# Linear attention's product with Wo in sixteen 32x32 tiles of the array, and two steps of the gated attention moved later

## The chip, the cores and the metric

The kernel runs on one core of a Trainium2 chip. The metric is the device time in microseconds of one execution; for the kernel before it is the median of three runs. Engines are named as the profile names them: PE is TensorE's matmul, PEld its weight load, DVE is VectorE, ACT is ScalarE, POOL is GpSimd, SP is SyncE. Times such as "at 93.2" are microseconds from the start of the profiled span.

## The reference, cut to what matters

Two layers on x of 2 x 1024 rows and 512 columns, all fp32: linear attention, a gated feed-forward with 4-bit weights, gated (chunked) linear attention, a feed-forward on the top half of the rows; a layer norm of the residual sum after each. The change touches the first and the third.

```python
# layer 0, linear attention: 16 heads of 32 columns
q = feature_map(proj(Wq))          # elu + 1, (b, h, t, d)
k = feature_map(proj(Wk))
v = proj(Wv)
kv = einsum('bhtd,bhte->bhde', k, v)
z = 1.0 / (einsum('bhtd,bhd->bht', q, k.sum(axis=2)) + 1e-06)
out = einsum('bhtd,bhde,bht->bhte', q, kv, z)
return out.reshape(b, t, c) @ Wo.T
...
# layer 1, gated attention: o comes from the chunked recurrence
go = o @ Wog.T + x @ Wig.T
on = o * rsqrt(mean(o * o) + EPS) * g_norm_w
return (on * silu(go)) @ Wo.T
```

## The kernel before, in words

Rows are worked in four blocks of 512 (two per batch), columns in four chunks of 128 (KC = 4). The kernel writes out the order of its matmuls by hand: generators are stepped by `run`, each step yields one or two products, and the lists given to `run` say what goes between them; `behind()` and `tc.issue_after` pin TensorE's order. On the other engines the compiler's scheduler orders the instructions, and each engine then runs its queue strictly in that order: an instruction that waits holds up all behind it.

**Linear attention** (first 230 us). `by_seven` (L304) makes a 512x512x512 projection with seven block products of 256 in place of eight (Strassen's scheme in Winograd's form): L315 is its matmul; the sums of blocks that it needs are `sums_of_weights` (L301) and VectorE operations at L322 to L324 and L339. One PSUM bank, `grow`, is added to by several products, so each reader of it has to be done before the next product may add. `elu1` (L270 to L272) is the feature map: two ScalarE passes and one on VectorE.

Per batch b, the kernel does not form v. It sums x^T k over the rows (`add_xk`, L366), a 512x512 array copied into G, and then:

- `values` (L417): Wv times G, only the four 128x128 blocks on the diagonal (four heads each), into the bank `vk`. VectorE multiplies it by a 0/1 mask, so that of each block only the four 32x32 squares of the heads remain (`vkm`, L420).
- `G_rows` (L430): for each chunk c one product of 128x128 by 128x512, `vkm[:, c]` with `Wo[:, c]`, into a bank `gp`; copies into G, two on VectorE and two on ScalarE (L431). G is now the weight that takes q to the output. Then VectorE makes the four block sums of G for the seven-product scheme (`sums_of_weights`, L301 again; tile names wdn, TG and T).
- `weigh` (L399 to L405): q is divided per row and head by q times the sum of k; six VectorE operations per 128 rows. The sum of k over the rows is spread over the partitions by a product with ones, and copied (`spread_ksum`, L391).
- `turned` (L446): q is transposed on TensorE in 128-column pieces (`qTp`, four transposes per 128 rows) and copied to `qT` by ScalarE.
- `o_products` (L461): qT times G by seven products, each added to the residual x by VectorE (L467). The sums S1, qS and A21 at L469 to L471 and A12 at L478 feed it.

Banks come from two rings of four or fewer: `mm` (projections) and `acc` (xk, qTp, gp, output products). Between these steps lies the unpacking of the 4-bit weights, one `job` at a time: a load on SyncE's queue, two VectorE operations (L236, L237; tile pk) and one ScalarE conversion (L240, tile wgu). For batch 1 the split of the next layer's input into two parts (`split_some`; x1Tp, x1Th by ScalarE, x1Tl by VectorE L211) lies there too. Wq arrives by DMA in the tile that the products read. `wdn` is the tile of the later feed-forward's down weights; its free chunks serve as room before it is filled.

**Gated attention** (545 to 745 us). Per block `scores`, `attend` and `gate` run. `gate` (L1180) makes go by seven products; L1215 and L1216 are two VectorE additions that empty its banks, L1224 another, `end` (L1194, L1197) applies silu and the norm weight. `finish_by_seven` (L1264, read by L1272) makes the product with the layer's own Wo (tile W1o) for the block before; the weight sums come from `sums_of_W1o` (four VectorE operations, L1241), the input sums from `sums_of_u` (L1249 to L1251). `gates.decayed` makes the decay factor of the second batch's keys: a product `ep` (L699) that needs ScalarE's logarithm l (L685), then exp (L702) and a VectorE product (L704); the next `scores` needs it for the states (`up`, L1112: one 128x32 by 128x512 product for each tile of rows, the results in four different strips of 32 partitions of one bank). The layer norm of a block takes row statistics on VectorE (L187, L188), a power on GpSimd (rs, L180) and the scaling on VectorE (L182). `x_sum` (L993) is a sum of the next block's input.

Of the kernel before, what the change touches and what calls it, by code (L numbers as in the profile page):

```python
# [21 lines left out]
P = 128  # L22
# [16 lines left out]
def _constants():  # L39
    t = np.arange(P)  # L40
    tt, ii = t[:, None], t[None, :]
    same = (tt // CH) == (ii // CH)
    mid = (ii // CH) * CH + CH // 2 - 1

    e1 = np.where(same & (tt > mid) & (tt <= ii), 1.0, 0.0)
    e1 -= np.where(same & (tt > ii) & (tt <= mid), 1.0, 0.0)
    e2 = np.where(ii < CH, (tt > ii) & (tt < CH), (tt >= CH) & (tt <= ii)) * 1.0
    e3 = (tt <= ii) * 1.0
    parts = {
        "ident": np.eye(P),  # L50
        "cm": -np.concatenate([e1, e2, e3], axis=1),
        "suf": -1.0 * (tt > ii),
        "caus": same & (tt <= ii),
        "tril": ii < tt,
        "heads": np.concatenate([(tt // 32) == (ii // 32), (tt // 32) == np.arange(4)[None, :]], axis=1),
        "one": np.ones((P, 1)),
        "place": tt + P * np.arange(4 * NB)[None, :],
        "mhalf": np.full((P, 4), -0.5),
    }
    at, n = {}, 0  # L60
    for name, a in parts.items():
        at[name] = (n, a.shape[1])
        n += a.shape[1]
    table = np.concatenate([np.asarray(a, np.float32) for a in parts.values()], axis=1)
    shift = (28 - 4 * (t % 8)).astype(np.int32)[:, None]
    return table, at, shift
# [6 lines left out]
def body(ctx: ExitStack, tc: tile.TileContext, a: dict, out: bass.AP):  # L73
# [13 lines left out]
    def bank(ring, name):  # L87
        i = rings[ring][turn_of[ring] % len(rings[ring])]
        turn_of[ring] += 1
        return psum.tile([P, 512], F32, tag=f"bank{i}", name=name)  # L90
# [3 lines left out]

    def acc_bank(name):
        return bank("acc", name)


    table = cpool.tile([P, _TABLE.shape[1]], F32, name="table")

    def const(name):
        at, n = _AT[name]
        return table[:, at : at + n]
# [11 lines left out]
    def load_w(dst, name):  # L115
        nc.sync.dma_start(out=dst, in_=a[name].rearrange("(k p) o -> p k o", p=P))
# [29 lines left out]
    nc.sync.dma_start(out=shift, in_=a["shift"])  # L146
    nc.sync.dma_start(out=table, in_=a["table"])
    load_x(1)
    load_w(Wq, "WqT")
    load_w(Wv, "WvT")  # L150
    load_w(Wo, "WoT")
    for blk in range(NB):
# [63 lines left out]
            nc.tensor.matmul(ps, lhs[:, k], w[:, k], start=start and k == 0, stop=stop and k == KC - 1)  # L216


    fp4 = ctx.enter_context(ExitStack())
    wfp4 = fp4.enter_context(tc.tile_pool(name="wfp4", bufs=1))  # L220
    wgu = wpool.tile([P, KC, 2 * I_FF], F32R, tag="big", name="wgu")
    wdn = wfp4.tile([P, NI, C], F32, name="wdn")
    gus = wfp4.tile([KC * FG, P], F16, name="gus")
    scale = wfp4.tile([P, KC * FG], F32, name="scale")
    s1 = ctx.enter_context(ExitStack())
    wk = s1.enter_context(tc.tile_pool(name="s1", bufs=2))
    dq = s1.enter_context(tc.tile_pool(name="dq", bufs=2))
# [25 lines left out]
            yield wdn[:, g], a["dn"][16 * g : 16 * (g + 1), :], a["dns"][g : g + 1, :], C  # L253

    to_unpack = unpacking()
    anchor = [None]

    def unpack_some(n):
# [6 lines left out]
    def elu1(dst, ps):  # L265

        e = wk.tile([P, C], F32, tag="e", name="e")
        if len(ps.shape) == 3:
            e = e.rearrange("p (r c) -> p r c", r=2)
        nc.scalar.activation(e, ps, AF.Relu, scale=-1.0)  # L270
        nc.scalar.activation(e, e, AF.Exp, scale=-1.0)
        anchor[0] = nc.vector.scalar_tensor_tensor(dst, ps, 0.0, e, ALU.max, ALU.add).ins  # L272


# [112 lines left out]
    def spread_ksum(b):  # L387

        sp_ = mm_bank("ksumb")
        with behind():  # L390
            last_pe[0] = nc.tensor.matmul(sp_, ones, ksum_of[b], start=True, stop=True).ins  # L391
        nc.scalar.copy(ksum_of[b], sp_)

    def weigh(blk, t):

# [14 lines left out]
    def values(b):  # L410

        vk = mm_bank("vk")
        with behind():
            for c in range(KC):
                cut = slice(c * P, (c + 1) * P)
                for k in range(KC):
                    ins = nc.tensor.matmul(vk[:, cut], Wv[:, k, cut], G_of[b][:, k, cut], start=k == 0, stop=k == KC - 1).ins  # L417
        last_pe[0] = ins
        vkm_of[b] = wk.tile([P, KC, P], F32, tag="vkm", name="vkm", bufs=1)
        nc.vector.tensor_mul(  # L420
            vkm_of[b],
            vk.rearrange("p (c d) -> p c d", c=KC),
            const("heads")[:, :P].unsqueeze(1).to_broadcast([P, KC, P]),
        )

    def G_rows(b):
        for c in range(KC):
            gp = acc_bank("gp")
            with behind():
                last_pe[0] = nc.tensor.matmul(gp, vkm_of[b][:, c], Wo[:, c], start=True, stop=True).ins  # L430
            (nc.scalar.copy if c % 2 else nc.vector.tensor_copy)(G_of[b][:, c], gp)  # L431

        room = wdn[:, 7:11] if b == 0 else place_w(3, "TG")
        rooms = slices(room, 0, 3)
        if b:

            rooms.append(pieces_of(wk.tile([P, 512], F32, tag="qT3", name="T3", bufs=1)))
        TG[b] = sums_of_weights(G_of[b], rooms), pieces_of(room[:, 3])
# [113 lines left out]
    def some_xk(blk, *part):  # L552
        return [lambda i=i: add_xk(blk, i) for i in part]
# [29 lines left out]
    for b in range(B):  # L583
        i, j = 2 * b, 2 * b + 1
        if b:
            run(
                k_products(i),
                turns(1, 0, 1) + job(1), job(1),
                turns(1, 2, 3) + some_o(1, 1) + job(1), some_o(1, 2) + job(1), some_o(1, 5) + job(1),
            )  # L590
        run(k_products(j), [], some_xk(i, 0, 1) + job(2), some_xk(i, 2) + job(1), some_xk(i, 3) + job(1), job(1 + b))
        if b == 0:
            Ts["q"] = sums_of_weights(Wq, slices(wdn, 0, 3))
        else:

            Tq = place_w(1, "Tq")
            for n in range(3):
                nc.scalar.copy(Tq[:, n], wdn[:, n])
            Ts["q"] = (*slices(Tq, 0, 2), Ts["q"][2], *slices(Tq, 2, 3))
            S_rooms[0] = pieces_of(Tq[:, 3])  # L600
        run(
            q_products(i, lambda t: weigh(i, t)), [],
            some_xk(j, 0, 1) + job(1 + b), some_xk(j, 2) + step(spread_ksum, b) + job(1), some_xk(j, 3) + job(1 + b),
        )
        if b == 0:
            xT[2] = load_xT(2)
        split = [step(split_some, n) if b else [] for n in range(4)]
        rings["free"] = (rings["sum"][(turn_of["sum"] + 1) % 2],)
        run(
            q_products(j, lambda t: None),  # L610
            step(values, b),
            turns(i, 0, 1) + split[0] + job(1 - b),
            step(G_rows, b) + split[1] + turns(i, 2, 3) + job(1 - b),
            some_o(i, 2) + split[2] + some_o(i, 1) + job(1 - b),
            step(all_free) + some_o(i, 1) + step(weigh, j, 0) + split[3] + some_o(i, 3) + step(weigh, j, 1) + some_o(i, 1),
        )
        if b == 0:
            xT[3] = load_xT(3)
# [447 lines left out]
    def scores(blk, gates, beside=None):  # L1066
# [7 lines left out]
        nc.tensor.transpose(tp[:, :P], of_tiles(gates.q, blk), ident)  # L1074
        nc.tensor.transpose(tp[:, P : 2 * P], of_tiles(gates.k, blk), ident)
        qp, kp = tp[:, :P], tp[:, P : 2 * P]
        own = const("heads")[:, P:]

        def over(x, n=P):
            return x.unsqueeze(1).to_broadcast([P, 4, n])  # L1080
# [163 lines left out]
    def sums_of_u():  # L1244

        A = uT[0].rearrange("p (m e) (s t) -> p m e s t", e=2, s=2)
        A11, A12, A21, A22 = (A[:, :, e, s] for s in range(2) for e in range(2))
        S1, S2 = (wk.tile([P, 512], F32, tag="sil", name=f"uS{i}", bufs=2).rearrange("p (m t) -> p m t", m=2) for i in range(2))
        nc.vector.tensor_add(S1, A21, A22)  # L1249
        nc.vector.tensor_sub(S2, S1, A11)  # L1250
        nc.vector.tensor_sub(A21, A11, A21)  # L1251
        return (A11, A12, A21, A22), (S1, S2)

    def finish_by_seven(blk, u, w):

# [398 lines left out]
        next(ending)  # L1654
    for blk in range(NB):
        if blk == 1 or blk == 2:
            sums = sums_of_u()
        if blk == 2:
            front(3, gates)
        if blk == 1:  # L1660
# [9 lines left out]
        if blk:  # L1670
            o_sum(blk)
            gating = gate(blk)
            if blk < 3:
                finishing = finish_by_seven(blk - 1, sums, W1o_sums)
                for n in range(2):
                    next(finishing)
                    next(gating)
                    if blk == 1 and n == 0:
                        with tc.issue_after(last_3[0]):
                            last_3[0] = gates.decayed(kd_room, jk.tile([P, 8, 32], F32, tag="junk", name="e3"))  # L1680
                next(finishing)
                scored = scored_rows(blk - 1)
            else:
                scored = finish(blk - 1)
                for _ in range(2):
                    next(gating)
# [6 lines left out]
            scores(blk + 1, gates)  # L1693
        if blk == 0:
            o_sum(0)
            with tc.issue_after(scored):
                W1o_sums = sums_of_W1o()
            nc.sync.dma_start(out=rw, in_=a["rw"].to_broadcast([P, C]))
            nc.sync.dma_start(out=b2, in_=a["b2"].to_broadcast([P, C]))
        other_sums(blk)  # L1700
# [123 lines left out]
```

## Time and profile before

| what | us |
|---|---|
| median of three runs | 966.21 (965.07 to 968.18) |
| profiled execution | 965.93 |
| its span, first to last instruction | 963.8 |
| TensorE busy (page) | 948.5 |
| VectorE busy (page) | 706.4 |
| ScalarE busy (page) | 290.8 |
| GpSimd busy (page) | 310.5 |
| mean granted TensorE clock | 0.999 of full speed |
| one pair of fp32 records of 512 columns, start to start (gp: 8 records from 83.29 to 86.73) | 0.86 |
| one product of the seven, four fp32 matmuls of 256 columns (start to start) | 1.73 |
| VectorE, one 128x512 fp32 operation: duration, and start to start | 0.68, 0.60 |
| ScalarE, one 128x512 copy out of PSUM: duration, and start to start | 0.59, 0.48 |

How to read it: the slices show an engine's busy share in tenths over 40 equal parts of the span (24 us each). A line of the timeline has the start, the length from the first start to the last end of a group, the engine, the line of the kernel, the operation, the tiles (written <- read), the form, the number of instructions, and in square brackets the engine's idle time before it with what ended it. Instructions of one engine overlap a little, so the step from start to start is shorter than the duration. An fp32 matmul shows as two records.

### The profile page before, as it was taken

What the parts mean: (1) busy time and instruction counts of PE and PEld (TensorE: products, weight loads), DVE (VectorE), ACT (ScalarE), POOL (GpSimd) and SP (SyncE); (2) the same over time, 40 slices, a digit from 0 to 9 for tenths busy, and PEclk for the clock granted to TensorE, in tenths of its full rate; (3) what the DMA queues carried; (4) which work ended last, traced back from release to release, by engine and by line L of the source; (5) the groups of instructions that cost most, each with busy time, mean ns of one, the idle gap of its engine ahead of it and who ended that gap; (6) DMA issues with size and microseconds to landing.
All of it is one profiled execution on the core that took longest, in us unless ns stands there. A gap on an engine that the chain in (4) does not pass through costs nothing. (4 is left out here: it accounts for less than half of the span.)

```text
span 963.8 us, 11530 instructions
## 1 busy us (share of the span) xinstructions
PE 948.5 (98%) x4261; PEld 753.1 (78%) x4261; DVE 706.4 (73%) x1343; ACT 290.8 (30%) x498; POOL 310.5 (32%) x278
## 2 busy tenths in 40 slices
PE   9999999999999999999999999999999999999996
PEld 6668876785788888888887866778758688888886
DVE  3569986887995676676669485584997795898635
ACT  2244333342552254245133323322122033220000
POOL 1110184003787445576557320101052021000022
PEclk9999999999999999999999999999999999999999
DMA  9622212200000000000011230000005302150011
GB/s 325 211 76 89 83 57 68 67 1 0 2 1 1 1 1 1 1 1 1 1 44 45 100 141 1 1 1 0 1 29 168 110 22 67 45 175 1 1 44 44
DMA packets 25978, 48.77 MB, mean 51 GB/s; under 512 B 4684, under 2 KB 6732, under 8 KB 25411
## 3 DMA queue, kind: packets, MB, share of 16 engines
q1 hardware_dynamic: 23283, 42.92, 13.2%
q0 software_dynamic: 1920, 4.22, 1.2%
q10 hardware_dynamic: 720, 0.92, 0.3%
q8 instruction: 33, 0.54, 0.2%
q14 instruction: 22, 0.18, 0.1%
HBM read 39.63 MB, written 10.52 MB: 52 GB/s over the span
## 5 line engine op out<-in xcount | busy, mean ns | idle before, releaser
L180 POOL TENSOR_TENSOR rs<-rs,table 128x4 f32<-128x4 f32 (+1 forms) x21 | 19.7, 937 | 296.8 <-DVE rs L179 296.5
L746 DVE SCALAR_TENSOR_TENSOR gate<-gatep,scale,gate 128x512 f32<-128x512 f32 x123 | 91.4, 743 | 6.3 <-PE gatep L735 5.9
L746 DVE SCALAR_TENSOR_TENSOR up<-upp,scale,up 128x512 f32<-128x512 f32 x112 | 83.1, 742 | 0.1
L735 PE MATMUL gatep<-x1Th,wgu 128*128 128x512 f32 x176 | 72.4, 411 | 0.6 <-DVE x1Tl L211 0.6
L735 PE MATMUL upp<-x1Th,wgu 128*128 128x512 f32 x176 | 70.4, 400 | 0.1
L735 PE MATMUL upp<-x1Tl,wgu 128*128 128x512 f32 x176 | 69.0, 392 | 0.0
L735 PE MATMUL gatep<-x1Tl,wgu 128*128 128x512 f32 x176 | 68.9, 392 | 0.0
L740 ACT ACTIVATE gate<-gatep,scale 128x512 f32<-128x512 f32 x41 | 28.3, 691 | 110.3 <-PE gatep L735 104.0
L936 POOL TENSOR_TENSOR h<-up,gate 128x512 f32<-128x512 f32 x30 | 39.2, 1308 | 68.3 <-ACT gate L935 63.0
L782 PE MATMUL P<-wdn,h 128*128 128x256 f32 x256 | 60.5, 379 | 0.0
L782 PEld LDWEIGHTS P<-wdn,h 128*128 128x128 f32 x256 | 48.4, 190 | 6.7
L1150 POOL TENSOR_TENSOR sum<-sum,sq 128x512 f32<-128x512 f32 x12 | 19.7, 1644 | 80.4 <-issue 66.3
L1180 PE MATMUL go<-big 128*128 128x256 f32 x192 | 43.7, 381 | 0.0
L366 PE MATMUL xk<-pair,x 128*128 128x512 f32 x96 | 42.7, 592 | 0.0
L187 DVE BATCH_NORM_STATS2 st<-x 128x6 f32<-128x512 f32 x64 | 42.0, 674 | 0.4
L735 PEld LDWEIGHTS upp<-x1Th,wgu 128*128 128x128 f32 x176 | 33.0, 188 | 11.6 <-DVE up L746 3.6
L1180 PEld LDWEIGHTS go<-big 128*128 128x128 f32 x192 | 35.9, 190 | 5.8 <-issue 1.2
L735 PEld LDWEIGHTS gatep<-x1Th,wgu 128*128 128x128 f32 x176 | 33.1, 188 | 9.2 <-DVE gate L746 2.1
L735 PEld LDWEIGHTS upp<-x1Tl,wgu 128*128 128x128 f32 x176 | 33.1, 188 | 6.4 <-issue 0.2
L735 PEld LDWEIGHTS gatep<-x1Tl,wgu 128*128 128x128 f32 x176 | 33.1, 188 | 6.0
L782 PE MATMUL P<-T,S 128*128 128x256 f32 x160 | 35.8, 379 | 0.0
L782 PEld LDWEIGHTS P<-T,S 128*128 128x128 f32 x160 | 30.3, 190 | 4.2
(489 smaller groups left out, 2266.4 us busy)
## 6 DMA issues: line engine op xcount, KB each, us to landing
pk<-in_gu SPq DMA_DIRECT2D x16, 352.0 KB, 3.7
x<-in_x SPq DMA_DIRECT2D x4, 1024.0 KB, 13.0
w<-in_w SPq DMA_DIRECT2D x1, 4096.0 KB, 14.6
xs<-picked SPq DMA_DIRECT2D x4, 1024.0 KB, 5.1
out<-x SPq DMA_DIRECT2D x4, 1024.0 KB, 4.3
w<-in_w SPq DMA_DIRECT2D x4, 1024.0 KB, 7.3
x0T<-in_xT SPq DMA_DIRECT2D x3, 1024.0 KB, 7.9
pk<-in_dn SPq DMA_DIRECT2D x11, 256.0 KB, 3.4
```

The costliest lines, as they stand in the source:

```text
L180: power = nc.gpsimd.tensor_tensor(rs[:, :n], rs[:, :n], const("mhalf")[:, :n], ALU.pow).ins
L187: nc.vector.bn_stats(st, x)
L366: ins = nc.tensor.matmul(acc_of[b][c], x_t[blk][:, i, c * P : (c + 1) * P], pairs_of["k", blk][i // 2][:, i % 2], start=blk % 2 == 0 and i ...
L735: ins = nc.tensor.matmul(ps, wgu[:, k, at * P : (at + 1) * P], x[:, k], start=x is parts[0], stop=x is parts[1]).ins
L740: nc.scalar.activation(acc, ps, AF.Copy, scale=s)
L746: last = nc.vector.scalar_tensor_tensor(acc, ps, s, acc, ALU.mult, ALU.add).ins
L782: last_p[0] = nc.tensor.matmul(cut, x(j)[:, r], w[:, j], start=j == 0, stop=j == NP - 1 and tail is None).ins
L936: hm = nc.gpsimd.tensor_mul(h.chunk(f), up, gate).ins
L1150: nc.gpsimd.tensor_add(sum2, sum2, sq)
L1180: ins = nc.tensor.matmul(ps[:, 256 * m : 256 * m + 256], w[:, k, m], b[:, k, 256 * half : 256 * half + 256], start=first and m == 0 and k ...
```

## The change

1. `G_rows`: instead of four 128x128 products with a masked `vkm`, sixteen products of 32x32 by 32x512. Head (c, j) takes partitions 32j to 32j+31 of `vkm[:, c]` and of Wo's chunk c, and writes partitions 32c to 32c+31 of the bank `gp[j]`. All four banks of the ring are taken at once. The mask goes; `vkm` is a plain ScalarE copy. G's four copies are all on ScalarE.
2. G's rows thereby stand in another order of heads. So q's columns do too: Wq is loaded into `wdn[:, 3:7]`, and `q_weights` copies it by ScalarE into the tile Wq with the columns in the new order; the copy of the spread ksum does the same. The first table column block of "heads" is no longer stored.
3. In the last product group of a batch the turns of q's last two row tiles go ahead of `G_rows`, and one unpacking job moves from beside it to the end of the group.
4. `sums_of_W1o` is issued at block 1 after `sums_of_u`, and no longer in block 0 after `scores`.
5. `gates.decayed` (`ep`) goes after the second pair of products of the finishing and the gate, and no longer after the first.

```diff
@@ _constants
-        "heads": np.concatenate([(tt // 32) == (ii // 32), (tt // 32) == np.arange(4)[None, :]], axis=1),
+        "own": (tt // 32) == np.arange(4)[None, :],
...
-    load_w(Wq, "WqT")
+    load_w(wdn[:, 3:7], "WqT")
...
@@ elu1
-        nc.scalar.activation(e, e, AF.Exp, scale=-1.0)
+        last_elu[0] = nc.scalar.activation(e, e, AF.Exp, scale=-1.0).ins
...
@@ spread_ksum
-        nc.scalar.copy(ksum_of[b], sp_)
+        nc.scalar.copy(ksum_of[b].rearrange("p (j c d) -> p c j d", j=4, c=4), by_heads(sp_))
+
+    by_heads = lambda x: x.rearrange("p (c j d) -> p c j d", c=4, j=4)
+
+    def q_weights():
+
+        for k in range(KC):
+            with tc.issue_after(last_elu[0]):
+                nc.scalar.copy(Wq[:, k].rearrange("p (j c d) -> p c j d", j=4, c=4), by_heads(wdn[:, 3 + k]))
...
@@ values
-        nc.vector.tensor_mul(
-            vkm_of[b],
-            vk.rearrange("p (c d) -> p c d", c=KC),
-            const("heads")[:, :P].unsqueeze(1).to_broadcast([P, KC, P]),
-        )
+
+        nc.scalar.copy(vkm_of[b], vk.rearrange("p (c d) -> p c d", c=KC))
 
     def G_rows(b):
+
+
+        gp = [acc_bank("gp") for _ in range(4)]
+        quad = lambda i: slice(32 * i, 32 * i + 32)
+        for j in range(4):
+            for c in range(KC):
+                with behind():
+                    last_pe[0] = nc.tensor.matmul(
+                        gp[j][quad(c)], vkm_of[b][quad(j), c, quad(j)], Wo[quad(j), c], start=True, stop=True
+                    ).ins
         for c in range(KC):
-            gp = acc_bank("gp")
-            with behind():
-                last_pe[0] = nc.tensor.matmul(gp, vkm_of[b][:, c], Wo[:, c], start=True, stop=True).ins
-            (nc.scalar.copy if c % 2 else nc.vector.tensor_copy)(G_of[b][:, c], gp)
+            nc.scalar.copy(G_of[b][:, c], gp[c])
...
@@ the loop over batches
-        run(k_products(j), [], some_xk(i, 0, 1) + job(2), some_xk(i, 2) + job(1), some_xk(i, 3) + job(1), job(1 + b))
+        q_ready = [] if b else step(q_weights)
+        run(
+            k_products(j), [],
+            some_xk(i, 0, 1) + job(2), some_xk(i, 2) + job(1) + q_ready, some_xk(i, 3) + job(1), job(1 + b),
+        )
...
             turns(i, 0, 1) + split[0] + job(1 - b),
-            step(G_rows, b) + split[1] + turns(i, 2, 3) + job(1 - b),
+            turns(i, 2, 3) + split[1] + step(G_rows, b),
             some_o(i, 2) + split[2] + some_o(i, 1) + job(1 - b),
-            step(all_free) + some_o(i, 1) + step(weigh, j, 0) + split[3] + some_o(i, 3) + step(weigh, j, 1) + some_o(i, 1),
+            step(all_free) + some_o(i, 1) + step(weigh, j, 0) + split[3] + some_o(i, 3) + step(weigh, j, 1) + some_o(i, 1)
+            + job(1 - b),
...
@@ sums_of_u
-        nc.vector.tensor_sub(A21, A11, A21)
-        return (A11, A12, A21, A22), (S1, S2)
+        ins = nc.vector.tensor_sub(A21, A11, A21).ins
+        return (A11, A12, A21, A22), (S1, S2), ins
...
@@ the loop over blocks of the gated attention
         if blk == 1 or blk == 2:
-            sums = sums_of_u()
+            *sums, summed = sums_of_u()
+            if blk == 1:
+                with tc.issue_after(summed):
+                    W1o_sums = sums_of_W1o()
...
-                    if blk == 1 and n == 0:
+                    if blk == 1 and n == 1:
                         with tc.issue_after(last_3[0]):
                             last_3[0] = gates.decayed(kd_room, jk.tile([P, 8, 32], F32, tag="junk", name="e3"))
...
             o_sum(0)
-            with tc.issue_after(scored):
-                W1o_sums = sums_of_W1o()
```

The pools that hold `wdn` and `wgu` are opened earlier, ahead of the loads, so that Wq can be loaded there.

## The prediction

> **What bounds the kernel now.** I read the page first (busy time, then slices), then what TensorE waited for, then the timelines around the three places that the change touches.
>
> ```profile
> PE 948.5 (98%) x4261; PEld 753.1 (78%) x4261; DVE 706.4 (73%) x1343; ACT 290.8 (30%) x498; POOL 310.5 (32%) x278
> ...
> PE   9999999999999999999999999999999999999996
> PEld 6668876785788888888887866778758688888886
> DVE  3569986887995676676669485584997795898635
> ```
>
> TensorE is busy from end to end; VectorE has slices at 9. So a microsecond of TensorE work removed counts only if what TensorE does next does not wait for VectorE instead. The list of TensorE's waits shows what it loses today:
>
> ```profile
> PE go L1180 <- DVE uT L1216: 2.9, 2, 2.3
> PE ep L699 <- ACT l L685: 1.8, 1, 1.8
> ...
> PE gatep L735 <- DVE x1Tl L211: 0.6, 1, 0.6
> ...
> PE grow L461 <- DVE x L467: 0.3, 1, 0.3
> ```
>
> The columns are total us, times, longest. The first two belong to the gated attention, and the change moves instructions around just these. The fourth is short but shows that linear attention runs in step with VectorE.
>
> **Part 1: the product with Wo (`G_rows`), sixteen small tiles.** Its cost now, and the nearest row to what replaces it (the `up` product, four tiles of 32 columns side by side):
>
> ```profile
> 83.29 3.60 PE L430 MATMUL gp<-Wo,vkm 128*128 128x512 f32 x8
> ...
> 558.49 1.07 PE L1112 MATMUL up<-x,big 128*32 128x512 f32 x8
> ...
> 559.49 0.59 PE L1060 MATMUL cp<-table,rw 128*128 128x384 f32 x1
> ```
>
> Both rows are four fp32 products of 512 columns, each two records. Side by side in four column groups they hold the array from 558.49 to 559.49, 1.0 us; one after another 3.44 (83.29 to 86.73). So column groups overlap fully: two rounds of 0.43 and about 0.1[...]. No row in this trace has tiles of 32 rows. Bounds for sixteen: four times 1.0 = 4.0 us if row groups don't overlap (0.6 more than now); about 1.1 if all do (2.3 less); 16 x 0.86 = 13.7 if nothing does. The Trainium skill (TensorE: Matmul & The Clock Gate, Part 3: Packing small matmuls) states 10.6 times for sixteen tiles of K=M=32, N=512: 13.7/10.6 = 1.3 us by that. I take two rounds, about 1 us, since the row shows its column half. Twice (one per batch): at most 4.7 us off TensorE.
>
> Where does that saving go? The compiled order of the changed kernel also puts the last two q turns (8 transposes, 0.87 us) ahead of the product, takes all four banks for it, and gives all four copies of G to ScalarE; VectorE loses two copies and the mask product (3 x 0.60 = 1.8 us per batch). Against this speaks a rule of the skill (TensorEngine Tiling (Array Packing), PSUM Bottleneck): the copies become the limit after packing, and both engines should share them. Here ScalarE copies follow each other at 0.48 us (87.41 and 87.89 for two qTp copies), so four take 2.0 us after the product, where today they run under its 3.44 us.
>
> Batch 0, followed by hand on the durations of the timeline. Without the mask product VectorE is 0.6 us earlier, so both pairs are weighed by 83.5 and the turns run 83.29 to 84.16. The product's fourth bank waits for the ScalarE copy of the last turn, done 0.63 + 0.48 + 0.59 us after the turns begin, 85.0; so TensorE leaves the product at about 86.0 (now 86.73, and the turns until 87.60): 1.6 us ahead. ScalarE next has an unpacking conversion that waits for VectorE until 85.6, so G's copies run 86.35 to 88.4 (now complete at 87.5). VectorE's sums of G then end at 90.2, three more operations of 0.6 stand before the first addition of the output (L467), which ends at 92.1. TensorE cannot overwrite that bank before:
>
> ```profile
> 92.47 0.68 DVE L467 TENSOR_TENSOR x<-x,grow 128x512 f32<-128x512 f32 x1
> ...
> 93.20 0.48 PE L461 MATMUL grow<-wdn,qS 128*128 128x256 f32 x1 [0.26 <-DVE x L467]
> ...
> 103.01 0.68 DVE L467 TENSOR_TENSOR x<-x,grow 128x512 f32<-128x512 f32 x1
> ...
> 103.74 0.48 PE L461 MATMUL grow<-G,wdn 128*128 128x256 f32 x1
> ```
>
> So it resumes at 92.2 instead of 93.2: 1.0 ahead. But before the fifth addition (now 103.01) the new order has four more weighing operations (0.16+0.55+0.60+0.08 = 1.4 us); from the elu at 97.5 (now 98.48, it hangs on TensorE) I get 103.45 for that addition, and TensorE at 104.2 instead of 103.74: the lead is gone, 0.4 behind. In the next block an unpacking job is now ahead of the sum qS (L470): it ends at about 120.1, TensorE wanted it at 119.85; 0.8 behind in all. Later VectorE has gaps, and TensorE runs through: +0.8 stays (bounds: -1.0, if the two orders cost nothing, to +2).
>
> Batch 1 the same way: turns at 195.79, split transposes, product 197.2 to 198.6, G's copies until 200.3 (now 200.0), first addition 204.5 (now 205.02), TensorE at 205.25 instead of 206.15; the stall before the gated unit (0.6, x1Tl) comes 0.8 earlier too. So -0.8 (bounds -2.3 to +0.7). **Part 1 in sum: about 0**, though 4.7 us of TensorE work go.
>
> **Part 2: q's columns reordered.** Wq lands in another tile and four ScalarE copies put it in place: 4 x 0.5 = 2 us at about 25.8. ScalarE's next work there is a copy at 31.74, so it is hidden. VectorE's sums of Wq (now from 22.99, 24.9, 25.5, 27.8) follow the copies and end at about 31.0; the next VectorE operation is at 31.69, TensorE needs them at 45.26 and later. Cost 0; with the cover gone 2 us. The reordered copy of ksum and the table without one column block (64 KB less): 0. One unpacking job later, with its load on SyncE: the load of the next xT goes ahead of one pk load, both early by far: 0.
>
> **Part 3: Wo's sums later.** Four VectorE operations (L1241) leave the stretch 565 to 578, where three of them fill with row statistics. The stall that they feed:
>
> ```profile
> 583.79 1.01 POOL L180 TENSOR_TENSOR rs<-rs,table 128x4 f32<-128x4 f32 x1
> 584.83 1.91 DVE L182 TENSOR_SCALAR x<-x,mv,rs 128x512 f32<-128x512 f32 x4 [1.37 <-POOL rs L180]
> ...
> 587.99 1.22 DVE L993 TENSOR_TENSOR big<-x2T 128x1024 f32<-128x1024 f32 x1
> 589.12 0.68 DVE L1216 TENSOR_TENSOR uT<-uT,go 128x512 f32<-128x512 f32 x1
> ```
>
> TensorE is ready at 587.45 and resumes at 589.85. With the new order the statistics end at 579.5, rs reaches GpSimd before ms (one power of 1.0 us less ahead of it), x is scaled 581.35 to 583.2, L1224 ends 583.95, its silu 585.05, then 2 x 0.66, 1.14 and 0.68: L1216 ends at 588.25. The stall shrinks from 2.4 to 0.9: **-1.55** (bounds -2.4 and 0). The four sums themselves (2.4 us) now follow `sums_of_u`, where VectorE stands idle from 597.7 to 605.0; TensorE needs the first at 614. Cost 0; 2.4 if that gap were gone.
>
> **Part 4: ep later.** At 611.55 TensorE has nothing left before ep, which waits for ScalarE's logarithm until 613.53. Now two Strassen products and one gate product go ahead, 6.9 us, and the logarithm is long done. What is late next is the read of the bank by L1272, at 611.9: a wait of 0.4. **-1.6** (bounds -2.0 and -0.8). Behind ep stand exp, one VectorE product and `up` at 628.9, some 8 us off; the ScalarE copy queued behind exp (the gate's second product) starts only at 624.6 today, and exp is over by 621. Cost 0.
>
> After 614 VectorE has gaps of 1 to 4 us (614.0, 618.8, 652.3, 667.1 by the timeline), and the routing chain starts from these products, so both gains travel to the end. Sum: 0 - 1.55 - 1.6 = -3.2 us. The profiled execution took 965.93 (span 963.8 and 2.1 around it), the median is 966.21; 966.2 - 3.2 = **963.0**.
>
> **Rivals.**
> A. TensorE bounds also in linear attention: the order on VectorE flexes enough that the 4.7 us arrive: 966.2 - 4.7 - 3.2 = 958.3. For it: only 0.3 us of TensorE waits there today. Against: VectorE is almost without a gap from 73 to 132. 20%.
> B. The forecast, 963.0, from 961.3 to 965. 50%.
> C. VectorE's queue takes more than the product gives: +2 in batch 0 and +0.7 in batch 1 (my upper bounds) leave 966.2 + 2.7 - 3.2 = 965.7; no change that shows. 20%.
> D. Slower: the sixteen tiles don't run side by side, because row groups of 32 bring no overlap and their order undoes that of the columns. Then each product lasts 13.7 instead of 3.44, +10.3; about 1 us per batch is swallowed by waits that go: +18 - 3.2, 981. Slower by over 0.3% begins where a product lasts (2.9 + 3.2)/2 = 3 us over today's 3.44, at some 6.5. For it: no row of 32-row tiles here. Against: `up` overlaps by four. 10%.
>
> That the change doesn't do what it says is part of A to D in one form: tiles that overlap by four only give 4.0 us and, with G later by up to 2 us per batch (+1.3 and +1.9 by the same steps), about 966.
>
> **Numbers.** A measurement of this kernel tells 0.3%, 2.9 us, from no change: the border is 963.3. A (20) and 32 of B's 50 lie below; 18 of B and C between; D above. Range 958.5 to 967.5: holds B, C and most of A; D and the rest of A are left out.
>
> **What would show it.** In the changed profile: gp 32 records within 1.0 to 2 us, with a wait for ScalarE inside; a wait of about 1.1 us at the third and 1.5 us at the seventh output product (L461's) for VectorE's additions; the stall of go on L1216 under 1.2; no wait of ep; Wo's sums between 594 and 599. Wrong if gp takes over 4 us, if TensorE doesn't wait for these additions (A), or if stalls of over 1 us appear after 620.

## The result and the profile after

The changed kernel took 963.17 us (median of 10 runs, 962.50 to 963.66), the kernel before 966.22 beside it (10 runs, 965.0 to 968.18). The ratio is 0.9969 with a 95% interval of 0.9959 to 0.9978. The forecast was 963.0. The profiled execution took 962.5 us, with a span of 960.7.

The page of the changed kernel, first line (busy us, share and instructions of each engine):

```profile
PE 945.7 (98%) x4309; PEld 751.2 (78%) x4309; DVE 704.7 (73%) x1337; ACT 295.5 (31%) x508; POOL 308.2 (32%) x278
```

TensorE has 2.8 us less to do, with 48 more instructions. What it waits for has changed. The list of TensorE's waits in the changed kernel (total us, times, longest):

```profile
PE grow L475 <- DVE x L481: 3.1, 4, 0.9
...
PE go L1199 <- DVE uT L1235: 1.0, 2, 0.6
...
PE gatep L754 <- DVE x1Tl L218: 0.6, 1, 0.6
PE grow L475 <- DVE qS L484: 0.6, 1, 0.6
PE grow L1283 <- DVE x L1291: 0.3, 1, 0.3
```

L475, L481 and L1235 are the old L461, L467 and L1216. The wait of ep for the logarithm (1.8) is gone and the one of go has fallen from 2.9 to 1.0: these are the two moves in the gated attention. But linear attention's output products, which lost 0.3 us to VectorE before, now lose 3.1 at L481 and 0.6 at qS.

The timeline of the changed kernel around the new product, in both batches, and where batch 0 ends:

```profile
83.53 1.07 ACT L460 COPY wdn<-qTp 128x512 f32<-128x512 f32 x2 [0.79 <-PE qTp L203]
83.86 1.86 PE L441 MATMUL gp<-Wo,vkm 32*32 32x512 f32 x32
...
86.00 2.03 ACT L445 COPY G<-gp 128x512 f32<-128x512 f32 x4
...
91.08 0.68 DVE L481 TENSOR_TENSOR x<-x,grow 128x512 f32<-128x512 f32 x1
...
91.81 1.99 PE L475 MATMUL grow<-wdn,qS 128*128 128x256 f32 x8 [0.72 <-DVE x L481]
...
131.34 1.99 PE L475 MATMUL grow<-G,wdn 128*128 128x256 f32 x8 [0.81 <-DVE x L481]
...
198.87 1.42 PE L441 MATMUL gp<-Wo,vkm 32*32 32x512 f32 x32
200.22 1.13 PE L317 MATMUL grow<-Tq 128*128 128x256 f32 x4
```

The product holds TensorE for 1.79 us in batch 0 (83.86 to the next product at 85.65), in which it waits for its fourth bank behind the ScalarE copies at L460, and for 1.35 in batch 1 (198.87 to 200.22). It was 3.44. The G copies, the first addition and the resumption of TensorE follow as forecast, until 131.34, where there is a wait that nobody forecast.

To see where time goes I compare **TensorE's place**: the start of the same instruction in the two traces, after minus before. The start of the kernel itself shifts with the first loads, by up to 1.5 us between the traces kept here, so steps count, not the absolute place. Parts are numbered as in the prediction: part 1 is points 1 and 3 of the change (the product and what moved around it), part 2 its point 2 (q's columns), part 3 its point 4 (the sums of W1o), part 4 its point 5 (ep). In these two traces:

| from, to (us) | step of the place | which part |
|---|---|---|
| start to 19 | -0.40 | first loads, no part of the change |
| batch 0, to 132 | +1.97 | 1 |
| batch 1, to 213 | -0.69 | 1 |
| 565 to 590 | -2.38 | 3 |
| 611 to 618 | -1.57 | 4 |
| sum | -3.07 | span 963.8 to 960.7 |

### The profile page after: what moved, and what is told of

The parts are those of the page before. It is cut to its first block, busy times and chain, and to the rows that moved or that the text cites. A ratio compares the mean times of both kernels' runs of the same rounds, so it can differ in the third digit from the quotient of the medians.

```text
span 960.7 us, 11628 instructions
## 1 busy us (share of the span) xinstructions
PE 945.7 (98%) x4309; PEld 751.2 (78%) x4309; DVE 704.7 (73%) x1337; ACT 295.5 (31%) x508; POOL 308.2 (32%) x278
## 4 chain that ended last, share of the span: by engine, by line
PE 81%; DVE 14%; ACT 2%; issue 2%; POOL 1%; POOLq 0%; ACTq 0%; DVEq 0%
PE P L801 13%; PE yp L1528 10%; PE upp L754 8%; PE gatep L754 8%; PE hp L1444 8%; PE xk L368 6%; PE go L1199 5%; PE grow L317 4%; PE P L317 3%; PE kp L541 1%; PE P L810 1%; PE ao L515 1%; PE ao L1317 1%; PE grow L1283 1%; DVE cmp L1368 1%
```

## The experiments

Two theories at the start. **Moves-pay**: parts 3 and 4 bring all of the gain and more, part 1 loses, because what the sixteen tiles save on TensorE comes back as waits for VectorE. **Tiles-pay** (the rival): the linear part brings its share, and the moves less. Each ratio is against runs of the kernel before in the same group. The groups e, c and d ran on three chips, so medians are compared within a group, and ratios across groups.

**e1: the kernel before with part 4 alone.**

```diff
-                    if blk == 1 and n == 0:
+                    if blk == 1 and n == 1:
```

> The kernel before with part 4 alone (ep after the second pair of products). Theory: TensorE loses its wait for ScalarE's logarithm (1.8 us) and gets a wait of 0.3 to 0.4 us for L1272 instead: 1.6 us less, 964.6. Rival 1 (the gain of the whole change comes from linear attention, parts 3 and 4 only shift waits): 0, 966.2. In the trace: no wait of ep, the step between the two programs' TensorE at that place 1.5 to 1.7 us, and nothing given back up to the end.

Measured: 966.41 (963.58 to 966.87, 12 runs) beside 967.55, ratio 0.999 (0.9981 to 0.9998). The trace shows the forecast's step at ep, -1.58, but the median shows less. The runs fall in two groups, three at 963.6 to 965.5 and nine at 966.0 to 966.9. The profiled execution shows why. Its timeline of TensorE after the stall that part 4 does not touch:

```profile
590.59 5.24 PE L1180 MATMUL go<-big,Wog 128*128 128x256 f32 x16 [2.34 <-DVE uT L1216]
```

and the same execution in two windows (us, then busy time and instructions of PE, PEld, DVE, ACT, POOL, then the granted clock, DMA share and GB/s):

```profile
586.00:590.30 4.30, 2.25 (x19) 1.77 (x17) 4.30 (x8) 2.05 (x4) 0.00 (x0) 1.00 0.00 0
590.30:593.70 3.40, 3.11 (x7) 2.52 (x8) 0.23 (x1) 0.63 (x1) 0.00 (x0) 0.50 0.00 0
```

For 3.4 us from the end of the wait on the granted clock is 0.50, and the group of sixteen matmuls takes 5.24 us where in the profiled execution of the kernel before, after the same stall, it takes 3.72:

```profile
589.85 3.72 PE L1180 MATMUL go<-big,Wog 128*128 128x256 f32 x16 [2.34 <-DVE uT L1216]
```

That is 1.5 us which some executions pay and some do not. The trace of e3, below, has it too: a granted clock of 0.50 for 3.41 us from 592.02, after the same wait of 2.34. The nine upper runs of e1 (median 966.65) are 1.3 us below the thirteen upper runs of the kernel before beside them (median 967.97); why nine of twelve were upper ones here stays open. d4 tests the cause.

**e2: the kernel before with part 3 alone** (`sums_of_W1o` at block 1 after `sums_of_u`; that part of the diff shown above).

> The kernel before with part 3 alone (Wo's sums of the gated attention after sums_of_u). As predicted: 1.55 us less, 964.7, the wait of go for L1216 at 0.9. As the trace of the changed kernel has it (TensorE steps from +0.88 to -1.50 between 560 and 590): 2.1 to 2.4 less, 963.9 to 964.1, the wait at 0.6. Rival 1: 0, 966.2.

Measured: 964.04 (962.41 to 964.23), ratio 0.9962 (0.9949 to 0.9975). TensorE's place steps by -2.40, as in the changed kernel and by 0.85 more than forecast.

**e3: the changed kernel without parts 3 and 4** (both undone, so parts 1 and 2 are left).

> The changed kernel with parts 3 and 4 taken back: linear attention's change alone (sixteen tiles, ScalarE's copies, q's order, turns, jobs). As predicted: 0, 966.2. As the trace of the changed kernel has it (TensorE at +0.88 at 207 and after, +1.28 with the 0.4 that came at the very start): slower by 0.9 to 1.3, 967.1 to 967.5. Rival 1 (the change gains here what TensorE no longer does, 4.7 us): 961.5.

Measured: 968.54 (967.05 to 969.47, 11 runs), ratio 1.001 (1.0001 to 1.0019): about 1.0 us slower than the kernel before. In the trace batch 0 costs +1.97 and batch 1 brings -0.69, net +1.3. Tiles-pay falls. (Runs with the half clock of e1 are in both sets, eight of 11 here and thirteen of 23 of the kernel before, told apart as in d4. With like beside like, e3 is slower by 0.8 or 0.9.) Its waits hold the new ones of linear attention beside the two old ones of the gated attention:

```profile
PE grow L475 <- DVE x L481: 3.1, 4, 0.9
PE go L1199 <- DVE uT L1235: 3.1, 3, 2.3
PE ep L718 <- ACT l L704: 1.8, 1, 1.8
```

**e4: the kernel before with parts 3 and 4, without 1 and 2.**

> The kernel before with parts 3 and 4, linear attention as it was. If linear attention's part costs 0.9 to 1.3: 962.1 to 962.5, faster than the changed kernel's 963.17. As predicted (that part is worth 0): 963.0. Rival 1: 966.2.

Measured: 962.40 (962.31 to 962.50), ratio 0.9951 (0.9939 to 0.9964); steps of -2.42 and -1.59. The two moves alone bring no less than the whole change. (c0 below, the changed kernel once more, gave 0.9954 on another chip: the two can't be told apart by these.)

**c0: the changed kernel once more**, to compare the next three with.

> The changed kernel once more, as the measure for the three beside it on this chip: 963.2. In the trace TensorE's start may move by up to 1 us with the first loads, the rest by under 0.3.

Measured: 963.47 (962.84 to 963.75), ratio 0.9954 (0.9941 to 0.9968).

**c1: VectorE's order.** If the saving of the tiles is lost because four weighing operations stand ahead of an addition that TensorE waits for, it must come back when both weighings go behind the additions.

```diff
-            step(all_free) + some_o(i, 1) + step(weigh, j, 0) + split[3] + some_o(i, 3) + step(weigh, j, 1) + some_o(i, 1)
+            step(all_free) + some_o(i, 1) + split[3] + some_o(i, 3) + step(weigh, j, 0) + step(weigh, j, 1) + some_o(i, 1)
```

> The changed kernel with the weighing of the next block's first q pair behind three more output products in the written order, so that VectorE makes the fifth addition to x before four of the weighing operations (and S1 and qS of the next block ahead of an unpacking step). Theory (VectorE's order gives the tiles' gain back in batch 0): the waits of the seventh output product (0.8 us at 103) and of qS (0.6 at 120) go or shrink below 0.3, and linear attention's part goes from +1.3 to about -0.3: 1.6 us less, 961.6. Rival (VectorE has too much work there whatever its order): the waits move to other additions, 963.2 within 0.5.

Measured: 961.10 (960.9 to 961.55), ratio 0.9933 (0.992 to 0.9947): 2.4 us under c0 on the same chip. Its waits:

```profile
PE grow L475 <- DVE x L481: 1.6, 2, 0.9
...
PE qTp L203 <- DVE z L412: 0.8, 2, 0.6
```

Two of the four waits at L481 are gone, the one at 131 among them, and that for qS as well; a new one of 0.8 has come, for the weighing that is now late. Parts 1 and 2 then bring -1.1 in the trace instead of +1.3. At 131 the order did more than move an addition: the VectorE operation that takes 1.75 us there is another one now and comes behind the addition (see the explanation below).

**c2: G's copies shared by ScalarE and VectorE**, as they were.

```diff
-            nc.scalar.copy(G_of[b][:, c], gp[c])
+            (nc.scalar.copy if c % 2 else nc.vector.tensor_copy)(G_of[b][:, c], gp[c])
```

> The changed kernel with G's copies shared between VectorE and ScalarE as before (two each). Theory (VectorE is what is late): two more operations of 0.6 us stand before VectorE's sums of G, the first output addition comes 0.5 to 0.8 us later in each batch, 0.5 to 1.5 us slower, 963.7 to 964.7. Rival (the copies after packing are the limit, so that both engines should share them): G is complete 1 us earlier, 1 to 2 us faster, 961.2 to 962.2.

Measured: 964.84 (964.2 to 965.09), 1.4 us over c0. The wait for the first addition grows from 0.9 to 1.6 by TensorE's place, in this list of its waits the total from 3.1 to 3.9:

```profile
PE grow L475 <- DVE x L481: 3.9, 4, 1.4
```

So the rule that the prediction weighed (the Trainium skill, TensorEngine Tiling (Array Packing), PSUM Bottleneck: let both engines empty the banks) does not hold here, and the measurement decides: between 82 and 93 in the changed kernel VectorE stands idle for 0.4 us in all, ScalarE for 2.07 in one gap alone. The size is less sure than the sign: by TensorE's place the shared copies cost 0.7 us at the first addition, and c2's trace has 0.5 more than c0's at the start and 0.3 more at 265, which no part touches.

**c3: the product ahead of the last two turns**, as it was, with the sixteen tiles kept.

```diff
-            turns(i, 2, 3) + split[1] + step(G_rows, b),
+            step(G_rows, b) + split[1] + turns(i, 2, 3),
```

> The changed kernel with the sixteen products ahead of the last two turns, as before the change. The turns then wait for ScalarE to empty two of G's banks (0.6 us) in place of the products that wait for the turns' copies; G is complete about 1 us earlier, and VectorE's order has the fifth addition of batch 0 ahead of most weighing again. If VectorE's order is what counts: 0.8 to 1.6 us less, 961.6 to 962.4. If the place of the product is what counts by itself (the turns' copies): 963.2 plus 0.3 to 0.6.

Measured: 961.59 (961.01 to 961.74), ratio 0.9936 (0.9923 to 0.995): 1.9 us under c0. In the trace batch 0 costs +0.7 and batch 1 brings -1.3.

**d1: c1 and c3 together.**

> The changed kernel with both the sixteen products ahead of the last turns and the weighing behind three more output products. If the two mend different waits (the one the first output addition of batch 1, the other the later additions of batch 0): 960.3 to 960.9, the best. If they mend the same one: 961.1 to 961.6, as each alone. More than 962 would speak against VectorE's order as the cause.

Measured: 961.27 (960.25 to 961.57), ratio 0.9942 (0.9928 to 0.9955). No better than c1 (0.9933): the two mend the same loss. TensorE now waits 1.3 us for the weighing (z), and still 1.9 in two waits for additions.

**d2: e4 (the old product, four full tiles) in c1's order.**

> The kernel before with parts 3 and 4 and the weighing behind three more output products, linear attention otherwise as it was (four masked products): tells how much of that order's gain needs the tiles. Theory (it only gives back what the tiles' kernel loses by its order): TensorE waits there for VectorE's additions by 0.3 only, so 0 to 0.5 less than the 962.4 of both moves alone, 961.9 to 962.4; the tiles are then worth about 1. Rival (the order alone is the gain): 960.0.

Measured: 964.77 (964.18 to 965.41, 11 runs), ratio 0.9977 (0.9968 to 0.9986). The expectation missed: the order that gains 2.4 us with the sixteen tiles loses with the old product, 0.9977 against 0.9951 for e4 (its trace puts the loss at 2.0 us of TensorE's time). Its waits show the same two kinds as c1, longer for the weighing:

```profile
PE qTp L196 <- DVE z L402: 1.3, 2, 0.7
...
PE grow L461 <- DVE x L467: 0.9, 2, 0.6
```

The wait of 0.6 for an addition has a cause that the written order does not show: the compiler ordered VectorE otherwise. In e4 the addition at 118.59 stands ahead of the sum qS; in d2 it comes at 120.61, behind qS (1.09 us instead of 0.68) and an unpacking step.

Beside d1, in the same group, the sixteen tiles with what goes with them (ScalarE's copies, q's order, one job moved) are thus worth 3.5 us with the weighing written late, where e3 has them cost 1.0 in the order of the change. In the traces of d1 and d2 linear attention has 2.4 of this; 0.4 is the start, and 0.5 lies between 300 and 500, which no part touches. And the old product is here in an order that does not suit it: each product in its better order, c1 beside e4, gives 0.9933 against 0.9951, some 1.7 us, with intervals that overlap. What the tiles are worth depends on VectorE's order, and the written order that suits one product does not suit the other.

**d3: GpSimd's additions out of the way.** The wait at 131 has a slow VectorE operation ahead of it. Here three of GpSimd's four additions to the sum of k are left out in one block, so that its sum of k for batch 1 is incomplete.

```diff
@@ sum_k
+            if blk == 2 and (t or r):
+                continue
```

> The changed kernel with three of GpSimd's four additions to the sum of k in block 2 left out (the sum of k of batch 1 is incomplete). Theory (the wait of 1.0 us at 131, which no step of the prediction had, comes from a VectorE elu that takes 1.75 in place of 0.68 us beside GpSimd's additions): the elu at 129 takes 0.7, the wait of the seventh product of block 1 falls from 1.0 below 0.2, 0.8 to 1.0 us less, 962.3. Rival (VectorE is behind anyway): the wait stays over 0.6, 963.0.

Measured: 961.89 (961.63 to 962.58), ratio 0.995 (0.9937 to 0.9964). The elu takes 0.68 and the wait at 131 is gone; TensorE is 1.24 us earlier at 207 than in c0. It is the trace that shows this: c0 ran on another chip, and the two ratios (0.995 and 0.9954) are not apart. The lines are shown with the explanation below.

**d4: the stall of the kernel before filled with work that nobody reads** (eight products of 128x128, so that TensorE is not idle there).

```diff
@@ gate, ahead of the last product of block 0
+            fill = mm_bank("fill")
+            turn_of["mm"] -= 1
+            for _ in range(8):
+                with tc.issue_after(last_3[0]):
+                    last_3[0] = nc.tensor.matmul(fill[:, :P], ident, ident, start=True, stop=True).ins
```

> The kernel before with eight products of 128 columns (1.7 us) that nobody reads, in the 2.5 us for which TensorE waits at 588. Theory (in about half the runs that idle stretch makes the clock fall to half for 3.4 us, which costs 1.6): the wait itself stays (the go product starts at 589.9 as before), the runs of 967.5 to 968.5 vanish, all lie within 965.0 to 967.0. Rival (the upper group has another cause): the runs fall into the same two groups.

Measured: 966.16 (965.89 to 966.86, 11 runs), ratio 0.9991 (0.9982 to 1.0), beside 967.21 (965.3 to 968.49) for the kernel before, 12 of whose 21 runs lie above 967.0. With the filling none does, though the critical product starts no earlier. TensorE's timeline:

```profile
587.30 1.95 PE L1238 MATMUL fill<-table 128*128 128x128 f32 x16
589.79 3.72 PE L1180 MATMUL go<-big,Wog 128*128 128x256 f32 x16 [0.55 <-DVE uT L1216]
```

It starts at 589.79, as in the kernel before (589.85), and takes 3.72, not 5.24. The mean granted clock of each run says the same. Of these 21 runs of the kernel before, the 12 above 967.0 have 0.996 or 0.997, and the other nine 0.998 or 0.999 but for one; of the 23 beside e1, the 13 above 967.5 have 0.996 or 0.997, and the ten below 966.9 have 0.998 or 0.999. So the upper group of runs is that in which the clock falls to half after the idle stretch.

## Why the forecast was right, and where two of its terms were not

The total was right to 0.2 us. The terms were not all: part 1 was put at 0 and costs 1.3 us in the trace, part 3 was put at -1.55 and brings 2.4. The two errors partly cancel, and by the runs they have one kind of cause. The parts bring -2.7 in the trace where -3.2 was forecast, and the start, which no part touches, the other -0.4: that the total fits so closely is in part luck. Beside c0, where six of ten runs of the kernel before lie above 967 (two of the ten beside the changed kernel's first runs), the changed kernel is 4.2 us ahead.

**The sixteen tiles overlap, by rows too: right.** I took about 1 us for the product without a wait and about 2 from 84.16 to 86.0 with the wait for the bank. It took 1.35 and 1.79, waits included. The 0.1 beyond the two rounds is a remainder of the sum; no run here shows what it is. Rival D falls, and so does the form in which only columns overlap (4.0).

**Part 1, batch 0, to 92: right.** TensorE was to resume 1.0 ahead; it does so at 91.81 instead of 93.20, 1.39 ahead, of which 0.40 is the start. The addition at fault was to end at 92.1 and ends at 91.76.

**The lead is gone by 104: right, the reason too.** With the start taken out the place is +0.2 there (forecast +0.4), after waits at the sixth and the seventh product. qS: forecast +0.8 in all, measured +0.9, after a wait of 0.6 for L484. c1 takes the cause away, the weighing ahead of the additions, and both waits go.

**"Later VectorE has gaps, and TensorE runs through": wrong.** This is the step that failed. At 131.34 TensorE waits (0.81, and its place steps by 1.1), and batch 0 costs +2.0, my upper bound, not +0.8. VectorE's timeline in the changed kernel, and GpSimd's beside it:

```profile
128.34 0.68 DVE L325 TENSOR_TENSOR rw<-Tk,x0T 128x512 f32<-128x512 f32 x1
128.94 1.75 DVE L274 SCALAR_TENSOR_TENSOR pair<-pair,e 128x512 f32<-128x512 f32 x1
130.61 0.67 DVE L481 TENSOR_TENSOR x<-x,grow 128x512 f32<-128x512 f32 x1
...
128.37 1.77 POOL L387 TENSOR_TENSOR ksum<-ksum,pair 128x512 f32<-128x512 f32 x1
```

The elu at L274 takes 1.75 us, not 0.68. It begins 0.57 us after GpSimd's addition and ends 0.55 after that ends (130.14). In d3, without the addition, the timeline of VectorE reads:

```profile
129.75 0.68 DVE L274 SCALAR_TENSOR_TENSOR pair<-pair,e 128x512 f32<-128x512 f32 x1
130.35 0.67 DVE L483 TENSOR_TENSOR x<-x,grow 128x512 f32<-128x512 f32 x1
```

The kernel before had a slow operation there too, but another one: a sum of input blocks (L324), behind the addition that TensorE wants. The elu (L272) took 0.68.

```profile
127.96 0.68 DVE L272 SCALAR_TENSOR_TENSOR pair<-pair,e 128x512 f32<-128x512 f32 x1
128.56 0.67 DVE L467 TENSOR_TENSOR x<-x,grow 128x512 f32<-128x512 f32 x1
...
129.66 1.75 DVE L324 TENSOR_TENSOR b<-x0T 128x512 f32<-128x512 f32 x1
...
129.43 4.63 POOL L385 TENSOR_TENSOR ksum<-ksum,pair 128x512 f32<-128x512 f32 x3
```

So it cost nothing, and in c1 it is that sum again (1.75 at 130.03), behind the addition. I had taken VectorE's durations as fixed; they depend on what GpSimd does at that moment, and the new order let the collision fall on an operation ahead of the addition. The Trainium skill (SBUF — State Buffer, Who interferes with whom) has this: a VectorE operation with two inputs in SBUF contends with a GpSimd operation that reads SBUF, and the order of issue decides which of them is blocked. The times agree here: GpSimd began first, and what is left after its end, 0.55, is about one operation alone. d3 shows that GpSimd's additions are the cause; that it is the port and no other thing shared by the two was not tried.

**Part 1, batch 1: right.** -0.8 forecast, -0.7 measured; the stall before the gated unit stayed as it was (0.6).

**Part 2 at no cost: right as far as it shows.** The place at 45, before part 1 begins, holds the start's -0.40 and no more.

**Part 3: the right place, too small.** The chain that I followed was right in kind: statistics, rs, scaling, L1235. But its front came 0.8 us sooner than I had it. GpSimd and VectorE in the timeline of the kernel before:

```profile
565.45 6.48 POOL L1150 TENSOR_TENSOR sum<-sum,sq 128x512 f32<-128x512 f32 x3 [11.04 <-ACT sq L1149]
...
568.75 2.05 DVE L1162 TENSOR_TENSOR big<-big 128x1024 f32<-128x1024 f32 x1
```

and of the changed kernel:

```profile
566.35 1.28 POOL L1169 TENSOR_TENSOR sum<-sum,sq 128x512 f32<-128x512 f32 x1 [11.04 <-ACT sq L1168]
568.08 1.27 POOL L1169 TENSOR_TENSOR sum<-sum,sq 128x512 f32<-128x512 f32 x1 [0.45 <-ACT sq L1168]
569.65 2.37 POOL L1169 TENSOR_TENSOR sum<-sum,sq 128x512 f32<-128x512 f32 x1 [0.30 <-ACT sq L1168]
...
569.68 1.21 DVE L1181 TENSOR_TENSOR big<-big 128x1024 f32<-128x1024 f32 x1
...
588.36 3.72 PE L1199 MATMUL go<-big,Wog 128*128 128x256 f32 x16 [0.43 <-DVE uT L1235]
```

Three of the four sums of W1o had stood beside GpSimd's additions. With them gone two of the three additions take 1.27 us, and are done before the VectorE operation at L1181 comes; it takes 1.21 in place of 2.05. That is 0.84 us more than the sums' own time. The third addition starts 0.03 us before it, and there the loss falls on GpSimd: 2.37 in place of 1.27. It is so in each of the profiles: 1.2 where part 3 is in, 2.05 where it is not (before, e1, e3, d4). No run takes GpSimd's additions away here, so for this place the cause is read from the timelines and from what d3 showed at 131, not tested. Of the step of -2.38, some 0.45 falls by 573, most of it where scores starts, and 1.95 at the stall, whose wait goes from 2.34 to 0.43. The sums themselves run from 596.1 to 598.7 in VectorE's gap, which lasts until 603.5: no cost, as forecast.

**Part 4: right.** -1.6 forecast, -1.57 to -1.59 measured in the changed kernel and in e1 and e4, with a wait of 0.3 (forecast 0.4) for L1291 in its place.

**Rivals.** A, all 4.7 us of TensorE's work arriving, is refuted by e3: the work goes and returns as waits for VectorE. By TensorE's place the new product gains 1.45 us in batch 0 and 1.9 in batch 1, and the delays behind it take 4.7 back (3.7 of this stands in the list of waits, all for VectorE; the list counts idle time alone). C was right for batch 0 (+2 was its number), wrong for batch 1 (+0.7, measured -0.7), and wrong on the total, since it kept part 3 at -1.55.

**A term that was in no sum.** The idle stretch of 2.4 us before go, which part 3 nearly removes, also costs the kernel before some 1.5 us of half clock (1.5 by TensorE's place in e1, 1.7 in e3) in about half of its executions. This is why its times scatter over 3 us and those of the changed kernel over 1.2, and part of why e1 shows less in its median than in its trace. Some runs of the changed kernel also show a mean clock of 0.997. That need not be a stall: in d1's profiled execution, at 0.997, the half clock lies in the last 4.9 us, in which TensorE has nothing left to do.

**Left open**: what makes the start vary; why the clock falls after the same stall in some executions and not in others; and whether a still better order of VectorE exists. The best version found is c1: below the changed kernel by 2.4 us on the same chip, and by its ratio (0.9933) below e4 (0.9951) too, though their intervals overlap.

## What to carry to other kernels

Where a second engine runs in step with the bounding one, work taken off the bounding engine can be worth nothing until the second engine's order is arranged for it: the same sixteen tiles cost 1 us in one order of VectorE, and brought 1.1 by the trace in another (c1). Before a sum is made of durations from a trace, look which of them were stretched by a neighbour: a VectorE operation with two inputs in SBUF took up to 1.1 us more beside a GpSimd addition here, and each reordering deals these collisions anew. A stall of TensorE can cost more than its length, when the clock falls behind it.

## What the runs showed of the hardware

- **Half clock after 2.4 us of idleness.** After the stall the granted clock was 0.50 for 3.41 us in some executions (the traces of e1 and e3) and 1.00 in others (that of the kernel before). The Trainium skill (TensorE: Matmul & The Clock Gate, Part 1) has a free-running window of 3413 ns and an idle window as the condition. The length agrees. The condition does not: here TensorE was idle for only some 2.4 us, with work on either side, and the measurement decides. Eight small products in the gap were enough to keep the clock: none of d4's 11 runs is in the upper group.
- **Tiles of 32 rows and 32 columns overlap in fp32.** In batch 1 the twelve records of the first round whose banks were free began within 73 ns (6.7 ns apart), and the second round 0.45 us after the first. Sixteen products of 32x32 by 512 columns took 1.35 us with a wait of 0.28, where four of 128x128 took 3.44.
- **VectorE and GpSimd.** 128x512 fp32 with two inputs in SBUF: 0.68 us alone, 1.75 beside a GpSimd addition of the same size that began 0.57 us earlier; 128x1024: 1.21 and 2.05. Where the two began within 0.03 us, VectorE kept its 1.21 and GpSimd's addition took 2.37 in place of 1.27.
